# Two column tiles for x_proj in a scan-plus-experts kernel, and an earlier due time for steps that give a PSUM bank back

## Chip, cores, metric

The kernel runs on one core of a Trainium2 chip. Its time is the device time of one execution in microseconds (us), as the median of the runs. All data are fp32.

## What is computed

Two layers work on x of shape (8, 384, 32, 32), with 1024 tokens per image. Layer 0 is a selective-scan block with a GELU MLP behind it; layer 1 is a mixture of four experts. Each has a group norm ahead and a residual around it. Cut to what matters:

```python
# layer 0, per image, t = tokens x channels (1024 x 384), after group norm and layer norm
xm, z = split(t @ in_proj_w.T)                    # 768 + 768
xc = silu(conv3(xm))                              # causal, 3 taps per channel
dbc = xc @ x_proj_w.T                             # 768 -> 24 + 16 + 16
dt, Bm, Cm = split(dbc, [24, 40])
dt = softplus(dt @ dt_proj_w.T + dt_proj_b)       # 24 -> 768
h_t = exp(dt*A) * h_(t-1) + (dt*xc) * Bm          # 16 states per channel, a scan over tokens
y = (sum_n h * Cm + xc * D) * silu(z)
x1 = x + gelu((y @ out_proj_w.T) @ w1.T + b1) @ w2.T + b2
# layer 1
out = x1 + sum_e coef_e * (relu(gn(x1) @ W1_e + b1_e) @ W2_e + b2_e)   # e = 0..3, two of them nonzero per token
```

The step that the change rewrites is `dbc = xc @ x_proj_w.T`: 768 inputs (six blocks of 128), 56 outputs.

## The kernel before

The tokens are cut into 16 chunks of T = 512, two to an image. Channels lie on the 128 partitions. A chunk of the scan has 24 rounds (6 blocks d of 128 channels, 4 groups s of states). In a round ScalarE makes four decays (`decay`, L790), GpSimd the drive (`drive`, L798), VectorE four scans (`scan`, L806), VectorE and GpSimd multiply the states by C (`read_out`, L810), and TensorE adds them over states into the PSUM tile y (`sum_states`, L832): four matmuls of 32 output columns side by side in the array, one per `tile_position`. Each fp32 matmul appears in the trace as two matmul instructions.

Around the scan of chunk i, the same engines do the dense work of its neighbours: in_proj and conv (L319, L338, L339), gate (L357) and x_proj (L378 to L396) of chunk i+1, out_proj (L500), the MLP (`hidden` L521, `second` L561) of chunks before, the scores of layer 1 (`scores`, L608) and the experts' first layer (`expert_lane`, L663), whose results go to DRAM. When the last scan is done, what is left of this dense work is finished, and then the experts' second layer runs for all chunks (L1147), 576 matmuls one after another.

The order of instructions is not written out by hand. A planner (`run`, `issue_one`, L938 to L976) walks through a modelled time at build time, with a clock per engine, and issues one step after another. The rounds of the scan are chains of `Step`s with dependences. The dense work consists of `Task`s, Python generators that yield an engine and a modelled duration for each step. On an engine, in this order, goes a side step that is late (`overdue`, L877: 2*(1+rank) us after it became ready, and 25 us more for a batch with table loads); then a due step of the scan; then a side step that fits into a gap (`fits`). On TensorE nothing counts as late. The plan fixes the order per engine, and the engines then wait for each other by semaphores.

Dense results go to one pool of four PSUM banks (`bank`, `free`, L211 to L216; BANKS = 4). A step that begins a matmul group in a fresh bank is issued only while fewer than four are held (L941). The bank is given back behind the step that empties it: an eviction by ScalarE or VectorE (`evict`, L482; `expert_evict`, L670), or the second of conv's two VectorE steps.

x_proj (L378) is planned at round 9 of the chunk before (L998). It takes a bank at its first matmul, adds the six blocks into rows 0 to 55 of it, one matmul per step, waits until the last dt projection of the chunk before is made (L387; the tile dbc has one buffer), copies the sum to SBUF on ScalarE (L391), gives the bank back and writes rows 24 to 55 to DRAM, from where they are read back spread over partitions (`load_rows`). The conv results come in two batches of SiLU, planned at rounds 6 and 9: blocks 0 to 2, and blocks 3 to 5. `delta` (L427) makes dt of one channel block out of dbc and is due from round 15 on.

Of the kernel before, what the change touches and what calls it, by code (L numbers as in the profile page):

```python
# [13 lines left out]
ALU = mybir.AluOpType  # L14
# [4 lines left out]
P = 128  # L19
# [6 lines left out]
ND = DI // P  # L26
# [5 lines left out]
BANKS = 4  # L32
# [3 lines left out]
MM, SUMS = 0.91, 1.05  # L36
ACT, COPY, TABLES = 0.70, 0.60, 2.6
SCAN, READ_A, DVE = 1.22, 1.30, 0.74
# [2 lines left out]
LAG = 0.07  # L41
SLACK = {"DVE": 0.35, "ACT": 0.15, "POOL": 0.3}
BATCH_SLACK = 0.5
RANK = 16.0
POLL = 0.5
DTR = 24
# [74 lines left out]
def layers(ctx, tc, io, ident, cmean, eps, dram, x1_dram, gn1, logits, r_dram, group_norm):  # L121
# [7 lines left out]
    V, S, G, PE = nc.vector, nc.scalar, nc.gpsimd, nc.tensor  # L129
# [27 lines left out]
    def weight(name, shape, queue=S):  # L157
        t = wp.tile(shape, F32, name="w_" + name)
        queue.dma_start(t, io[name])
        return t  # L160
# [5 lines left out]
    w_x = weight("x_proj", [P, ND, DTR + 2 * NS])  # L166
# [33 lines left out]
    xc, zs, dtr, dxr, dbc, bc_dram, bt, ct, gn = {}, {}, {}, {}, {}, {}, {}, {}, {}  # L200
# [5 lines left out]
    psq_user = []  # L206


    held = [0]

    def bank(name):  # L211
        held[0] += 1
        return ps_g.tile([P, T], F32, name=name, tag="g")

    def free():
        held[0] -= 1  # L216

    class Stream:

# [158 lines left out]
    def x_proj(i):  # L378
        g = None
        m = DTR + 2 * NS  # L380
        for d in range(ND):
            while (i, d) not in xc:
                yield "-", POLL
            yield "bank" if d == 0 else "PE", MM
            g = bank("g_x") if d == 0 else g
            PE.matmul(g[0:m, :], lhsT=w_x[:, d, :], rhs=xc[i, d], start=(d == 0), stop=(d == ND - 1))
        while i > 0 and (i - 1, ND - 1) not in projected:  # L387
            yield "-", POLL
        yield "ACT", COPY
        sums = p1.tile([m, T], F32, name="dbc")  # L390
        S.copy(sums, g[0:m, :])  # L391
        yield "-", 0
        free()
        bc_dram[i] = dram.tile([2 * NS, T], F32, name=f"bc_dram{i}")
        nc.sync.dma_start(bc_dram[i], sums[DTR:m, :])
        dbc[i] = sums  # L396
# [14 lines left out]
    def load_b(i, s):  # L411
        begin(load("b", bt, i, 0, s), rank=0)
# [66 lines left out]
    tt, x1, hs, pre, ready = {}, {}, {}, {}, {}  # L479
    scored, waiting = set(), set()  # L480

    def evict(g, us, engine, then, done=lambda: None):  # L482
        yield engine, us
        then(g)
        yield "-", 0
        free()
        done()

    def out_proj(i):
        while (i, ND - 1) not in finished or i - 1 in tt:  # L490
            yield "-", POLL
        t = p1.tile([P, J, T], F32, name="tt")
        for j in range(J):
            g = None
            for k in range(2):
                yield "bank" if k == 0 else "PE", 3 * MM
                w = w_out.take("out_proj", 2 * j + k)
                g = bank("g_out") if k == 0 else g
                for d in range(3):
                    PE.matmul(g, lhsT=w[:, d, :], rhs=xc[i, 3 * k + d], start=(k + d == 0), stop=(k == 1 and d == 2))  # L500

            begin(evict(g, COPY, "ACT", lambda g, j=j: S.copy(t[:, j, :], g),
                        lambda j=j: ready.setdefault(i, []).append(j)), rank=1, after=now[0] + 3 * MM)
        yield "-", 0
        out_done.add(i)
        while len(ready.get(i, [])) < J:
            yield "-", POLL
        tt[i] = t

    def hidden(i, us):  # L510
        while i not in tt:
            yield "-", POLL
        for u in us:
            while len(waiting) == HID:
                yield "-", POLL
            yield "bank", 3 * MM
            waiting.add((i, u))
            w = w_1.take("mlp_w1", u)
            g = bank("hid")
            for j in range(J):  # L520
                PE.matmul(g, lhsT=w[:, j, :], rhs=tt[i][:, j, :], start=(j == 0), stop=(j == J - 1))  # L521

            def then(g, u=u):
                h = pre[i, u] = ph.tile([P, T], F32, name="h")
                S.activation(h, g, AF.Identity, bias=b1[:, u:u + 1])
            begin(evict(g, ACT, "ACT", then), rank=1, after=now[0] + 3 * MM)
            if u % 3 == 2:
                begin(gelus(i, range(u - 2, u + 1)))

# [19 lines left out]
    def second(i, half):  # L549
        us = range(half * NF // 2, (half + 1) * NF // 2)  # L550
        for j in range(J):
            g = None
            for k in range(2):
                mine = [(i, us[3 * k + n]) for n in range(3)]
                while not all(m in hs for m in mine) or i not in x1:
                    yield "-", POLL
                yield "bank" if k == 0 else "PE", 3 * MM
                w = w_2.take("mlp_w2", 4 * j + 2 * half + k)
                g = bank("acc") if k == 0 else g
                for n in range(3):  # L560
                    PE.matmul(g, lhsT=w[:, n, :], rhs=hs[mine[n]], start=(k + n == 0), stop=(k == 1 and n == 2))  # L561

            def then(g, j=j):
                y = x1[i][:, j, :]
                if half == 0:
                    V.scalar_tensor_tensor(y, g, b2[:, j:j + 1], y, ALU.add, ALU.add)
                    return
                V.tensor_tensor(y, g, y, ALU.add)
                b = i // NH
                if b not in stats:  # L570
                    stats[b] = p2.tile([P, NH * J, 6], F32, name="st1")
                V.bn_stats(stats[b][:, (i % NH) * J + j, :], y)
                summed[i] = summed.get(i, 0) + 1
                if summed[i] == J:
                    nc.sync.dma_start(x1_dram[i], x1[i])
                    if i % NH == NH - 1:
                        begin(scores(i // NH))
            begin(evict(g, 2 * DVE if half else DVE, "DVE", then), rank=1, after=now[0] + 3 * MM)
        yield "-", 0
        waiting.difference_update((i, u) for u in us)  # L580

# [68 lines left out]
    def expert_lane():  # L650

        for i in range(NCH):
            if i < NCH - 1:
                yield from load_xn(i, pxn)
            while i not in xns:
                yield "-", POLL
            xn = xns.pop(i)
            for u in range(E * J):
                yield "bank", 3 * MM
                w = w_e.take("e_w1", u)  # L660
                h = bank("e_hid")
                for j in range(J):
                    PE.matmul(h, lhsT=w[:, j, :], rhs=xn[:, j, :], start=(j == 0), stop=(j == J - 1))  # L663

                begin(expert_evict(h, i, u), rank=1, after=now[0] + 3 * MM)
            yield "-", 0

    writing = []
# [1 line left out]
    def expert_evict(h, i, u):  # L670
        while len(writing) == 2:
            yield "-", POLL
        writing.append((i, u))
        yield "ACT", ACT
        r = pr.tile([P, T], F32, name="r")
        S.activation(r, h, AF.Relu, bias=e_b1[:, u:u + 1])  # L676
        yield "-", 0
        free()
        nc.sync.dma_start(r_dram[i][u], r)
        yield "-", DMA  # L680
        writing.remove((i, u))
# [174 lines left out]
    class Task:  # L856
        def __init__(self, steps, rank, after):
            self.steps, self.rank, self.end, self.engine = steps, rank, after, None
            self.advance()

        def advance(self):
            last = self.engine
            self.engine, us = next(self.steps, (None, 0))
            self.at = "PE" if self.engine == "bank" else "ACT" if self.engine == "batch" else self.engine
            self.us = us
            self.ready = self.end + (us if self.engine == "-" else 0) + (LAG if self.engine != last else 0)
# [7 lines left out]
        def urgency(self):  # L874
            return self.rank * RANK + self.ready

        def overdue(self):  # L877
            return self.ready + 2 * (1 + self.rank) + (25 if self.engine == "batch" else 0)

    now, clock = [0.0], {"PE": 0.0, "DVE": 0.0, "ACT": 0.0, "POOL": 0.0}  # L880
    tasks, ends, steps, chains = [], {}, {}, {e: [] for e in clock}

    def begin(*new, rank=2, after=None):
        tasks.extend(Task(t, rank, now[0] if after is None else after) for t in new)

    def chain(engine, items):

# [37 lines left out]
    def fits(t):  # L925
# [9 lines left out]
        wait = max(0, now[0] - t.ready) if t.engine == "batch" else 0  # L935
        return end + ACT + 2 * LAG <= starved() + (BATCH_SLACK + wait / 10 if t.engine == "batch" else 0)

# [294 lines left out]
```

## Time and profile before

| | us |
|---|---|
| median of 3 runs (lowest, highest) | 3879.05 (3877.36, 3880.08) |
| the profiled execution's own time | 3874.76 |
| its span | 3873.0 |
| mean granted TensorE clock | 0.965 |
| x_proj's 96 matmuls (L386): busy | 95.4 |
| the sums over states (L832), 384 groups of four: busy | 462.9 |
| copies dbc<-g_x (L391), 16 | 9.1 |
| the experts' second layer (L1147), 576 matmuls: busy | 494.6 |

Busy time is the time in which an engine works, on a row or in a window. "Idle before, releaser" tells what an engine's next instruction waited for. TensorE's ends are modelled, so the distance from one start to the next is the better measure there. A share of busy time is a mean over stages with different limits, so it is read by stage.

### The profile page before, as it was taken

What the parts mean: (1) busy time and instruction counts of PE and PEld (TensorE: products, weight loads), DVE (VectorE), ACT (ScalarE), POOL (GpSimd) and SP (SyncE); (2) the same over time, 40 slices, a digit from 0 to 9 for tenths busy, and PEclk for the clock granted to TensorE, in tenths of its full rate; (3) what the DMA queues carried; (4) which work ended last, traced back from release to release, by engine and by line L of the source; (5) the groups of instructions that cost most, each with busy time, mean ns of one, the idle gap of its engine ahead of it and who ended that gap; (6) DMA issues with size and microseconds to landing.
All of it is one profiled execution on the core that took longest, in us unless ns stands there. A gap on an engine that the chain in (4) does not pass through costs nothing.

```text
span 3873.0 us, 35214 instructions
## 1 busy us (share of the span) xinstructions
PE 3628.0 (94%) x10294; PEld 1374.8 (35%) x10294; DVE 3008.6 (78%) x3081; ACT 2385.4 (62%) x3714; POOL 2773.1 (72%) x1070
## 2 busy tenths in 40 slices
PE   6769798999999999999999999999999998999999
PEld 2213233333333333333333333333333343444444
DVE  3899899999989998989799979898888802055554
ACT  4758586868787878787777777777776632200000
POOL 2899899999989998999899989899889800000000
PEclk8869898999999999999999999999999998999999
DMA  4334455555546565555555456555555536555553
GB/s 132 123 124 160 150 167 186 169 196 179 202 157 207 179 202 167 202 187 180 177 197 190 162 178 214 174 183 178 179 167 187 177 99 205 199 196 196 187 179 109
DMA packets 374804, 677.90 MB, mean 175 GB/s; under 512 B 40508, under 2 KB 151484, under 8 KB 372436
## 3 DMA queue, kind: packets, MB, share of 16 engines
q1 hardware_dynamic: 372448, 675.31, 52.1%
q8 instruction: 83, 1.36, 0.1%
q14 instruction: 109, 0.89, 0.1%
q10 hardware_dynamic: 2164, 0.34, 0.0%
HBM read 535.90 MB, written 139.59 MB: 174 GB/s over the span
## 4 chain that ended last, share of the span: by engine, by line
PE 49%; DVE 16%; ACT 13%; POOL 9%; DMA 6%; issue 5%; SPq 1%; POOLq 0%; ACTq 0%; DVEq 0%
PE acc L1147 13%; PE e_hid L663 8%; PE acc L561 7%; DVE da_A L806 6%; POOL du L798 6%; PE hid L521 6%; PE g_in L319 6%; DVE du L806 4%; PE y L832 4%; ACT da_A L790 4%; PE g_out L500 4%; POOL du L810 2%; DVE du L810 2%; ACT da_B L790 2%; DMA mlp_w<-in_mlp_w 1%
## 5 line engine op out<-in xcount | busy, mean ns | idle before, releaser
L798 POOL TENSOR_TENSOR du<-dxr,b 128x2048 f32<-128x2048 f32 x384 | 1739.2, 4534 | 84.0 <-PE y L832 56.6
L810 POOL TENSOR_TENSOR du<-du,c 128x1024 f32<-128x1024 f32 x384 | 905.6, 2359 | 114.5 <-DVE du L806 84.5
L790 ACT ACTIVATE da_A<-dtr_a,w_a_log 128x512 f32<-128x512 f32 x768 | 529.5, 689 | 254.0 <-DVE carry L815 106.6
L790 ACT ACTIVATE da_B<-dtr_b,w_a_log 128x512 f32<-128x512 f32 x768 | 525.3, 684 | 217.5 <-DVE du L806 203.9
L319 PE MATMUL g_in<-xt,in_proj 128*128 128x512 f32 x1152 | 554.3, 623 | 44.2 <-DMA in_proj<-in_in_proj 16.9
L663 PE MATMUL e_hid<-xn,e_w 128*128 128x512 f32 x1152 | 534.9, 607 | 36.3 <-DMA xn<-xn_dram 16.0
L521 PE MATMUL hid<-tt,mlp_w 128*128 128x512 f32 x1152 | 536.4, 608 | 27.7 <-DMA mlp_w<-in_mlp_w 22.7
L806 DVE TENSOR_TENSOR_SCAN du<-da_B,carry,du 128x512 f32<-128x512 f32 x384 | 487.6, 1270 | 91.3 <-ACT da_B L790 77.5
L561 PE MATMUL acc<-h,mlp_w 128*128 128x512 f32 x1152 | 541.4, 608 | 17.4 <-DMA mlp_w<-in_mlp_w 10.8
L806 DVE TENSOR_TENSOR_SCAN da_A<-da_A,carry,du 128x512 f32<-128x512 f32 x384 | 491.4, 1280 | 56.9 <-ACT da_A L790 54.1
L832 PE MATMUL y<-du,sel 128*32 128x512 f32 x3072 | 462.9, 625 | 73.5 <-DVE du L810 28.8
L806 DVE TENSOR_TENSOR_SCAN du<-da_B,du 128x512 f32<-128x512 f32 x384 | 464.3, 1209 | 76.4 <-ACT da_B L790 51.0
L806 DVE TENSOR_TENSOR_SCAN da_A<-da_A,du 128x512 f32<-128x512 f32 x384 | 467.7, 1218 | 43.7 <-ACT da_A L790 38.5
L1147 PE MATMUL acc<-r,w_e_w 128*128 128x512 f32 x1152 | 494.6, 592 | 0.0
L810 DVE TENSOR_TENSOR du<-da_A,c 128x1024 f32<-128x1024 f32 x384 | 468.0, 1219 | 8.9
L319 PEld LDWEIGHTS g_in<-xt,in_proj 128*128 128x128 f32 x1152 | 216.9, 196 | 370.6 <-issue 258.1
L663 PEld LDWEIGHTS e_hid<-xn,e_w 128*128 128x128 f32 x1152 | 217.1, 193 | 330.5 <-issue 270.5
L521 PEld LDWEIGHTS hid<-tt,mlp_w 128*128 128x128 f32 x1152 | 214.2, 192 | 330.8 <-issue 276.7
L561 PEld LDWEIGHTS acc<-h,mlp_w 128*128 128x128 f32 x1152 | 213.6, 192 | 323.7 <-issue 277.4
L1147 PEld LDWEIGHTS acc<-r,w_e_w 128*128 128x128 f32 x1152 | 218.9, 190 | 275.5 <-issue 275.5
L500 PE MATMUL g_out<-xc,out_proj 128*128 128x512 f32 x576 | 269.4, 604 | 0.3 <-ACT r L676 0.3
L676 ACT ACTIVATE r<-e_hid,w_e_b 128x512 f32<-128x512 f32 x192 | 129.6, 680 | 194.3 <-PE e_hid L663 127.2
(125 smaller groups left out, 2929.7 us busy)
## 6 DMA issues: line engine op xcount, KB each, us to landing
dxr<-dxr_dram SPq DMA_DIRECT2D x384, 256.0 KB, 4.7
mlp_w<-in_mlp_w SPq DMA_DIRECT2D x384, 192.0 KB, 3.9
dtr_b<-dtr_dram SPq DMA_DIRECT2D x192, 256.0 KB, 4.1
dtr_a<-dtr_dram SPq DMA_DIRECT2D x192, 256.0 KB, 3.3
r_dram<-r SPq DMA_DIRECT2D x192, 256.0 KB, 2.8
r<-r_dram SPq DMA_DIRECT2D x64, 768.0 KB, 4.6
in_proj<-in_in_proj SPq DMA_DIRECT2D x192, 192.0 KB, 3.6
e_w<-in_e_w SPq DMA_DIRECT2D x192, 192.0 KB, 3.5
```

The source lines that it names most:

```text
L319: PE.matmul(g, lhsT=w[:, j, :], rhs=xt[i][:, j, :], start=(j == 0), stop=(j == J - 1))
L500: PE.matmul(g, lhsT=w[:, d, :], rhs=xc[i, 3 * k + d], start=(k + d == 0), stop=(k == 1 and d == 2))
L521: PE.matmul(g, lhsT=w[:, j, :], rhs=tt[i][:, j, :], start=(j == 0), stop=(j == J - 1))
L561: PE.matmul(g, lhsT=w[:, n, :], rhs=hs[mine[n]], start=(k + n == 0), stop=(k == 1 and n == 2))
L663: PE.matmul(h, lhsT=w[:, j, :], rhs=xn[:, j, :], start=(j == 0), stop=(j == J - 1))
L676: S.activation(r, h, AF.Relu, bias=e_b1[:, u:u + 1])
L790: S.activation(out, dtr[i, d][pair][:, j % 2, :], AF.Exp, scale=neg_a[:, d, j, s:s + 1])
L798: G.tensor_tensor(du[r], dxr[i, d], wide(bt[i, s].unsqueeze(1), [P, Q, T]), ALU.mult)
L806: V.tensor_tensor_scan(a if j < 2 else b, a, b, start, ALU.mult, ALU.add)
L810: engine.tensor_tensor(du[r][:, js, :], h, wide(ct[i, s].unsqueeze(1), [P, 2, T]), ALU.mult)
L832: PE.matmul(y[j * m:(j + 1) * m, :], lhsT=sel, rhs=h[:, j, :], start=False, stop=(s == NG - 1), tile_position=(0, j * m), skip_group_check ...
L1147: PE.matmul(acc[j], lhsT=e2[:, e, d, j, :], rhs=r[:, d, :], start=(e + d == 0), stop=(e + d == E + J - 2))
```

## The change

x_proj is done in three pairs of matmuls. Blocks d and d+3 run as two column tiles of one bank: block d into rows 0 to 55 (tile position 0), block d+3 into rows 64 to 119 (tile position 64). A pair is one step with a modelled duration of 1.2 us and starts only when both its blocks are there. The two partial sums are joined behind: ScalarE copies the first to SBUF as before, then a new VectorE step adds the second to it, reading it from PSUM, and the bank is given back after that.

The planner is changed too. A task counts the banks that it holds (`holds`); where one task fills a bank and another empties it, the count is handed on (`current[0].holds -= 1`, `holds=1`). While all four banks are held, a step of a task that holds one is late 0.5 us after it is ready (SHORT), instead of 2*(1+rank) us.

```diff
+SHORT = 0.5
...
-    held = [0]
+    class Nobody:
+        holds = 0
+
+    held, current = [0], [Nobody]
 
     def bank(name):
         held[0] += 1
+        current[0].holds += 1
         return ps_g.tile([P, T], F32, name=name, tag="g")
 
     def free():
         held[0] -= 1
+        current[0].holds -= 1
...
-        for d in range(ND):
-            while (i, d) not in xc:
+
+        for d in range(ND // 2):
+            while (i, d) not in xc or (i, d + ND // 2) not in xc:
                 yield "-", POLL
-            yield "bank" if d == 0 else "PE", MM
+            yield "bank" if d == 0 else "PE", 1.2
             g = bank("g_x") if d == 0 else g
-            PE.matmul(g[0:m, :], lhsT=w_x[:, d, :], rhs=xc[i, d], start=(d == 0), stop=(d == ND - 1))
+            for k in range(2):
+                PE.matmul(g[k * P // 2:k * P // 2 + m, :], lhsT=w_x[:, k * ND // 2 + d, :], rhs=xc[i, k * ND // 2 + d],
+                          start=(d == 0), stop=(d == ND // 2 - 1), tile_position=(0, k * P // 2))
         while i > 0 and (i - 1, ND - 1) not in projected:
             yield "-", POLL
         yield "ACT", COPY
         sums = p1.tile([m, T], F32, name="dbc")
         S.copy(sums, g[0:m, :])
+        yield "DVE", DVE
+        V.tensor_tensor(sums, g[P // 2:P // 2 + m, :], sums, ALU.add)
         yield "-", 0
         free()
...
+            current[0].holds -= 1
             begin(evict(g, COPY, "ACT", lambda g, j=j: S.copy(t[:, j, :], g),
-                        lambda j=j: ready.setdefault(i, []).append(j)), rank=1, after=now[0] + 3 * MM)
+                        lambda j=j: ready.setdefault(i, []).append(j)), rank=1, after=now[0] + 3 * MM, holds=1)
...
         def __init__(self, steps, rank, after):
             self.steps, self.rank, self.end, self.engine = steps, rank, after, None
+            self.holds = 0
             self.advance()
 
         def advance(self):
             last = self.engine
+            outer, current[0] = current[0], self
             self.engine, us = next(self.steps, (None, 0))
+            current[0] = outer
...
         def overdue(self):
+            if self.holds and held[0] == BANKS:
+                return self.ready + SHORT
             return self.ready + 2 * (1 + self.rank) + (25 if self.engine == "batch" else 0)
...
-    def begin(*new, rank=2, after=None):
-        tasks.extend(Task(t, rank, now[0] if after is None else after) for t in new)
+    def begin(*new, rank=2, after=None, holds=0):
+        for t in new:
+            tasks.append(Task(t, rank, now[0] if after is None else after))
+            tasks[-1].holds += holds
```

The handing on is done in the same two lines in `hidden`, `second` and `expert_lane`. No other instruction is added or taken away; the order on each engine comes from the planner again.

More of the change, by code (lines that the diff above doesn't have):

```diff
@@ L525, in then @@
                 S.activation(h, g, AF.Identity, bias=b1[:, u:u + 1])
-            begin(evict(g, ACT, "ACT", then), rank=1, after=now[0] + 3 * MM)
+            current[0].holds -= 1
+            begin(evict(g, ACT, "ACT", then), rank=1, after=now[0] + 3 * MM, holds=1)
             if u % 3 == 2:
@@ L577, in then @@
                         begin(scores(i // NH))
-            begin(evict(g, 2 * DVE if half else DVE, "DVE", then), rank=1, after=now[0] + 3 * MM)
+            current[0].holds -= 1
+            begin(evict(g, 2 * DVE if half else DVE, "DVE", then), rank=1, after=now[0] + 3 * MM, holds=1)
         yield "-", 0
@@ L663, in expert_lane @@
                     PE.matmul(h, lhsT=w[:, j, :], rhs=xn[:, j, :], start=(j == 0), stop=(j == J - 1))
-                begin(expert_evict(h, i, u), rank=1, after=now[0] + 3 * MM)
+                current[0].holds -= 1
+                begin(expert_evict(h, i, u), rank=1, after=now[0] + 3 * MM, holds=1)
             yield "-", 0
```

## Prediction, made blind

> **What bounds the kernel now.** I read the busy shares first, then cut the span into stages at the points where the work changes, then took TensorE's waits by stage, then single instructions. The stages (columns: window in us, its length, then busy us and count of each engine, granted clock, DMA share, GB/s):
>
> ```profile
> 0.00:700.00 700.00, 567.71 (x1565) 190.41 (x1566) 581.18 (x601) 475.94 (x758) 590.40 (x245) 0.87 0.46 150
> 700.00:3090.00 2390.00, 2306.24 (x6973) 852.21 (x6972) 2135.97 (x2125) 1830.97 (x2840) 2182.53 (x825) 0.99 0.55 184
> 3090.00:3373.00 283.00, 259.45 (x606) 113.47 (x606) 29.51 (x58) 77.76 (x116) 0.20 (x1) 0.95 0.48 157
> 3373.00:3873.00 500.00, 494.57 (x1153) 218.69 (x1151) 261.97 (x299) 0.69 (x1) 0.00 (x0) 1.00 0.50 179
> ```
>
> To 700 us the scan leads: GpSimd and VectorE are busy and TensorE idles 132 us, because the dense work of later layers isn't there yet. From 700 to 3090 TensorE is busy 96.5%; VectorE idles 254 us. From 3090, where the last sum over states ends, TensorE alone works off what is left of the MLP and the experts' first layer, and from 3373 the experts' second layer. So after 700 us a microsecond of TensorE work is nearly a microsecond of span, wherever the planner puts it. Its waits between 700 and 3090 (us in total, times, longest):
>
> ```profile
> PE hid L521 <- DMA mlp_w<-in_mlp_w: 22.7, 10, 5.7
> PE acc L561 <- DMA mlp_w<-in_mlp_w: 6.7, 5, 2.6
> PE g_in L319 <- ACT da_B L790: 6.4, 3, 2.9
> PE mu L281 <- ACT r L676: 4.7, 2, 3.1
> PE y L832 <- POOL du L810: 4.4, 5, 1.5
> ```
>
> All lines of this view together come to 84 us: 37 for DMAs, 8.5 of y for the scan, 38 of dense matmuls for a ScalarE or VectorE step, mostly one that gives back a bank or makes an input. TensorE hardly waits for the scan here. It is the other way round, in GpSimd's waits of the same window:
>
> ```profile
> POOL du L810 <- DVE du L806: 74.1, 44, 6.2
> POOL du L798 <- PE y L832: 52.2, 27, 6.3
> ```
>
> The second line is the scan held up by TensorE.
>
> **What a matmul costs**, from TensorE's timeline (start, length, engine, line; two instructions are one fp32 matmul):
>
> ```profile
> 1499.83 1.92 PE L386 MATMUL g_x<-xc,w_x_proj 128*56 128x512 f32 x4
> 1501.68 1.06 PE L832 MATMUL y<-du,sel 128*32 128x512 f32 x8
> 1502.68 1.07 PE L386 MATMUL g_x<-xc,w_x_proj 128*56 128x512 f32 x2
> 1503.67 5.42 PE L521 MATMUL hid<-tt,mlp_w 128*128 128x512 f32 x12
> 1509.02 1.06 PE L832 MATMUL y<-du,sel 128*32 128x512 f32 x8
> ```
>
> From start to start, two x_proj matmuls take 1.85, one takes 0.99: 0.86 each and 0.13 once per group. Four y matmuls in four column tiles take 1.00, as much as one x_proj matmul. Six 128-column matmuls take 5.35. The last stage gives the bare price, 494.6/576 = 0.859.
>
> **Part 1, x_proj in pairs.** Removed: six matmuls in a row per chunk, 6 x 0.86. Added: three pairs. No row shows two tiles of 64 columns. The bounds are the y row (tiles run fully side by side: 0.86 a pair) and two x_proj matmuls (no overlap: 1.72). I take 0.86, since y runs four tiles with four moving tensors in that time. That is 3 x 0.86 = 2.58 us less per chunk, 41 in all.
>
> [...] The row: a group in another mode costs 0.13 at its end, and three dense matmuls take 2.67 instead of 2.58 ahead of a y, 0.09 at its start; together 0.22. [...] But the x_proj of before pays the 0.13 already. In the instruction order, which is fixed at build time, its 96 matmuls stand in 53 groups; the 48 pairs stand in 32. Counted over all kinds, TensorE changes between kinds 922 times before the last y in the old order and 887 times in the new, 35 x 0.12 = 4 us less. I take the row.
>
> x_proj of chunks 0 to 3 lies ahead of 700 us, where TensorE waits for the scan. Those 4 x 2.58 = 10 us only turn into idle. What counts is 31 + 4 = 35 us.
>
> **Part 2, the VectorE add.** Nearest row: x<-acc,x (L568), a sum of PSUM and SBUF into SBUF, 676 ns; 16 x 0.68 = 11 us on VectorE, covered by its 254 us of idle time. If that cover is gone it is 11 on the path. The add also waits for ScalarE's copy, and scans are queued behind it. VectorE's longest wait for a decay here is 5.0 us, so I bound this at 0 to 16 x 3 = 48, and take 0 beyond the 11, as the planner puts the add behind the copy's planned end. For what follows, the copy stands near round 14.2 of the chunk before (15.2 in the old order) and the first dt near round 16: 1.8 rounds of 7.8 us cover 0.7 us, and the write of B and C and their loads on SP's queue come no later. Only chunk 0 at the start has no cover: 0.7 us.
>
> **Part 3, banks.** Pairs need blocks 3 to 5, so x_proj's bank is taken at round 12 instead of 9 to 11, and given back at 14 to 15 instead of 14 to 16. One bank of four is held for about 2 rounds rather than 4 to 5. With SHORT, evictions go ahead of scan steps while all four are held. Both let the planner fit in more dense work before the scan ends. Behind the last y the old order has 285 dense matmuls (18 out_proj, 45 hid, 57 acc, 165 e_hid), the new one 186 (18, 36, 36, 96). So 99 x 0.859 = 85 us of work goes out of the stage 3090 to 3373 and into the scan's stage.
>
> *Stage behind the scan:* -85, if its idle time stays. TensorE waits 23.4 us there, for xn (12.0) and e_w (11.4). In the new order no expert group stands between hid and acc of the last half, nor beside the group norm's small matmuls, as some do now: about 2.7 for a GELU batch with its table load, and 10 to 12 from the last acc over statistics, norm and logits. But then e_hid of chunks 14 and 15 starts when xn lands, about when it does now, and the wait for e_w behind the big loads lies inside that. I take the same 23; bounds 10 and 45.
>
> *Scan's stage, 700 to 3090:* TensorE's load goes from 2306 to 2306 + 85 - 35 = 2356. Idle time on top: 37 for DMAs and 8.5 for the scan stay; of the 38 for banks and inputs I let half go, 19. That makes 2421, +31. With none gone +50; with all gone +12.
>
> *What the late rule may cost:* ScalarE's side work between two decays is lumpier in the new order. Summed over the rows' durations, what exceeds 4 us between two decays comes to 205 us instead of 168, with ten lumps of 8 to 13 us against one. Decays feed scans, so up to 37 us go onto the scan chain. The scan's own pace is 184 to 187 us per chunk where it leads (drives before 700 us), 12.5 chunks make 2300 to 2340; with 37 it is 2340 to 2377, still under 2421. So I put it at nothing beyond the idle time kept above; without that cover it is 37.
>
> **Sum** on the profiled execution: 31 - 85 + 0.7 = -53. Span 3873 - 53 = 3820, own time 3821.6 (1.8 lie around the span). The median of the runs is 4.3 above that execution's own time, so I predict 3826.
>
> **Rivals.**
> - *More absorbed:* most bank waits go, the scan's stage grows by 12 or less: -73 and beyond, under 3806. For it: the shorter hold, and chunks that take 192 to 199 us while TensorE idles up to 8% in some 100 us slices. Against it: mlp_w's 29 us come from DMA and nothing here changes them. 0.16.
> - *Lumps or unoverlapped tiles eat part:* the 37 us come on top of TensorE's load (-53 + 37 = -16, 3863), or pairs cost 1.72 (-53 + 31 = -22, 3857). The y row speaks against the second. Between 3845 and 3871: 0.17.
> - *Slower:* one mechanism, the eviction lumps on ScalarE at the conv and SiLU batches of each chunk (rounds 8 to 16). A lump starves VectorE's scans, the sums over states come late, and TensorE, in order, stands before y with dense work queued behind, as it does before 700 us. Price: 50 of load with no idle saved, 37 of lumps, 11 of the add: 98 on the scan's stage, against 85 gained: +13, 3892. It decides from 85 us of growth, 6.8 us per chunk. For it: VectorE waits 186 us for decays already. Against it: y waits for the scan only 8.5 us there, so the scan has room. 0.09.
>
> **How the numbers follow.** The likeliest case, 3806 to 3845, has 0.54 and gives 3826. About 0.2% (8 us) is what a measurement can tell from no change; 3871 to 3887 gets 0.04. Faster is 0.54 + 0.16 + 0.17 = 0.87, slower 0.09. The range from 3788 to 3868 leaves out 0.06 below (all idle for banks gone and a tail with 10 of waits) and 0.14 above.
>
> **What would show it.** Right: L386's successor has 96 matmuls with about 50 us busy, 3 pairs start to start in 2.7; the last y ends near 3120, the experts' second layer starts near 3320; dense waits for ScalarE and VectorE about 19 between 700 and the last y. Wrong: pairs at 1.7; y waiting tens of us for GpSimd or VectorE after 700 (slower rival); the stage behind the scan longer than 210 us, which would mean that the chain of the last chunk is bare.

## The result and the profile after

| | before | after |
|---|---|---|
| median us (lowest, highest), 4 runs each | 3878.2 (3877.11, 3880.08) | 3820.39 (3816.69, 3823.5) |
| ratio, 95% interval | | 0.985 (0.9833 to 0.9867) |
| span of the profiled execution | 3873.0 | 3816.7 |
| TensorE busy / span less busy | 3628.0 / 245.0 | 3586.5 / 230.2 |
| x_proj's matmuls, busy | 95.4 | 53.9 |
| last y starts; experts' second layer starts | 3088.8; 3373.0 | 3123.4; 3316.7 |

The change gains 58 us; 3820 was measured where 3826 had been predicted. The stages of the changed kernel, cut at the same events (window, length, then busy us and count of TensorE's matmuls, its weight loads, VectorE, ScalarE, GpSimd; granted clock, DMA share, GB/s):

```profile
0.00:700.00 700.00, 558.34 (x1537) 187.95 (x1538) 577.48 (x597) 467.55 (x745) 579.66 (x242) 0.86 0.45 147
700.00:3124.00 2424.00, 2357.83 (x7198) 882.29 (x7196) 2157.32 (x2151) 1852.72 (x2884) 2195.33 (x828) 0.99 0.57 188
3124.00:3317.00 193.00, 176.07 (x417) 77.47 (x410) 24.72 (x51) 56.51 (x86) 0.21 (x1) 0.93 0.46 153
3317.00:3817.00 500.00, 494.24 (x1152) 218.50 (x1150) 262.00 (x299) 0.69 (x1) 0.00 (x0) 1.00 0.50 179
```

The scan's stage has grown by 35 us and carries 52 us more TensorE work; the stage behind it has shrunk from 283 to 193; the last is the same. The pairs, in TensorE's timeline (start, length; four instructions are one pair):

```profile
1707.19 1.07 PE L394 MATMUL g_x<-xc,w_x_proj 128*56 128x512 f32 x4
1708.19 1.07 PE L847 MATMUL y<-du,sel 128*32 128x512 f32 x8
1709.19 1.12 PE L444 MATMUL g_dt<-dbc,w_dt_proj 24*128 24x512 f32 x2
1710.24 1.93 PE L394 MATMUL g_x<-xc,w_x_proj 128*56 128x512 f32 x8
1712.10 1.12 PE L325 MATMUL g_in<-xt,in_proj 128*128 128x512 f32 x2
```

One pair takes 1.00 from start to start and two take 1.86, where one and two single matmuls took 0.99 and 1.85: the two tiles run side by side. Of TensorE's waits from 700 us to the last y, the longest:

```profile
PE e_hid L677 <- DMA e_w<-in_e_w: 14.4, 5, 3.6
PE acc L574 <- DMA mlp_w<-in_mlp_w: 5.7, 5, 2.0
PE y L847 <- ACT y L840: 5.0, 4, 1.8
PE g_x L394 <- ACT z L363: 4.8, 1, 4.8
PE g_logits L635 <- ACT h L537: 3.7, 1, 3.7
```

All lines of this view come to 66 us (84 before): 23 for DMAs (37), 10.6 of y (8.5), 32 for ScalarE and VectorE (38). y's waits have grown by 2 us only, so the scan keeps up. And behind the last y, the longest:

```profile
PE e_hid L677 <- DMA xn<-xn_dram: 6.6, 1, 6.6
PE g_logits L635 <- ACT x L628: 2.7, 2, 1.8
PE acc L574 <- ACT h L549: 2.7, 1, 2.7
PE gn_m L100 <- DVE gn_mv L97: 1.9, 1, 1.9
```

The last chunk's chain, which had expert groups in its gaps before, now shows its waits, but they are small: 17 us in this stage against 23.

### The profile page after: what moved, and what is told of

It reads as the page before. It is cut to its first block, busy times and chain, and to the rows that moved or that the text cites. A ratio compares the mean times of both kernels' runs of the same rounds, so it can differ in the third digit from the quotient of the medians.

```text
span 3816.7 us, 35175 instructions
## 1 busy us (share of the span) xinstructions
PE 3586.5 (94%) x10294; PEld 1366.2 (36%) x10294; DVE 3021.5 (79%) x3097; ACT 2377.5 (62%) x3714; POOL 2775.2 (73%) x1070
## 4 chain that ended last, share of the span: by engine, by line
PE 49%; DVE 17%; ACT 15%; POOL 7%; issue 5%; DMA 5%; SPq 2%; ACTq 0%; POOLq 0%; DVEq 0%
PE acc L1169 13%; PE e_hid L677 8%; DVE da_A L821 7%; PE hid L533 7%; PE acc L574 6%; PE g_in L325 6%; POOL du L813 5%; DVE du L821 5%; PE y L847 4%; ACT da_A L805 4%; PE g_out L511 3%; DVE du L825 2%; POOL du L825 2%; ACT da_B L805 2%; ACT L205 2%
## 5 line engine op out<-in xcount | busy, mean ns | idle before, releaser
L533 PE MATMUL hid<-tt,mlp_w 128*128 128x512 f32 x1152 | 528.2, 603 | 14.0 <-DMA mlp_w<-in_mlp_w 7.1
L847 PEld LDWEIGHTS y<-du,sel 128*32 128x32 f32 x3072 | 68.3, 109 | 411.3 <-issue 96.5
```

Source lines behind the costliest of these rows:

```text
L847: PE.matmul(y[j * m:(j + 1) * m, :], lhsT=sel, rhs=h[:, j, :], start=False, stop=(s == NG - 1), tile_position=(0, j * m), skip_group_check ...
```

## The experiments

Every ratio is to the kernel before, run on the same chip. "Idle" is span less TensorE's busy time, in the profiled execution; "rest" is TensorE's busy time without x_proj, the same matmuls in every row. The profiled execution is not always near the median: those of due_only and after_null are 6 us faster, that of one_tile_no_add 6 us slower.

| run | median us | ratio (95% interval) | idle | rest | clock |
|---|---|---|---|---|---|
| before | 3878 | 1 | 245.0 | 3532.6 | 0.965 |
| changed kernel | 3820 | 0.985 (0.9833 to 0.9867) | 230.2 | 3532.6 | 0.966 |
| one_tile | 3838 | 0.9899 (0.9885 to 0.9912) | 224.1 | 3519.6 | 0.969 |
| one_tile_no_add | 3838 | 0.9901 (0.9887 to 0.9914) | 226.4 | 3520.9 | 0.967 |
| due_only | 3848 | 0.9925 (0.9912 to 0.9937) | 220.6 | 3526.1 | 0.967 |
| late_start | 3859 | 0.9957 (0.9944 to 0.9971) | 235.5 | 3527.1 | 0.967 |
| pairs_only | 3870 | 0.9979 (0.9971 to 0.9987) | 263.6 | 3549.1 | 0.962 |
| pairs_only_null | 3857 | 0.9947 (0.9935 to 0.996) | 249.8 | 3549.8 | 0.962 |
| short_2 | 3830 | 0.9882 (0.9868 to 0.9895) | 233.0 | 3537.7 | 0.963 |
| three_held | 3856 | 0.9948 (0.9935 to 0.996) | 259.5 | 3541.6 | 0.962 |
| after_null | 3827 | 0.9874 (0.9859 to 0.9889) | 230.2 | 3534.2 | 0.966 |
| before_null | 3880 | 1.0009 (1.0 to 1.0017) | 249.6 | 3533.0 | 0.966 |
| add_five_psum | 3861 | 0.9959 (0.9945 to 0.9972) | 251.5 | 3555.1 | 0.964 |
| add_five | 3933 | 1.0143 (1.0127 to 1.0158) | 297.1 | 3579.8 | 0.955 |

**one_tile: TensorE's time alone.** The order on all engines is the changed kernel's, instruction for instruction.

```diff
-                PE.matmul(g[k * P // 2:k * P // 2 + m, :], ..., start=(d == 0), stop=(d == ND // 2 - 1), tile_position=(0, k * P // 2))
+                PE.matmul(g[0:m, :], ..., start=(d + k == 0), stop=(d + k == ND // 2))
-        V.tensor_tensor(sums, g[P // 2:P // 2 + m, :], sums, ALU.add)
+        V.tensor_tensor(sums, g[0:m, :], sums, ALU.max)
```

> The plan and the order are those of the changed kernel, but each pair's two matmuls go into the same column tile, one behind the other, and VectorE's step reads that tile again (a maximum of equal values, the same duration). Only TensorE's time per pair differs. Theory A (after 700 us TensorE's work is the span; a pair saves 0.86): 12 chunks x 2.58 = 31 us slower than the changed kernel, 3851, with x_proj busy about 95. Theory B (the gain comes from the order and the banks, and the time saved on TensorE falls into its waits): 0 to 10 us slower, 3820 to 3830.

0.49% or 19 us slower than the changed kernel, between the two theories. x_proj's group and the scan's stage:

```profile
L394 PE MATMUL g_x<-xc,w_x_proj 128*56 128x512 f32 x192 | 92.6, 618 | 12.6 <-ACT xc L379 4.9 <-ACT z L363 4.1 <-ACT h L537 3.6
```

```profile
700.00:3141.00 2441.00, 2383.77 (x7194) 889.53 (x7196) 2157.80 (x2151) 1854.34 (x2883) 2195.28 (x828) 0.99 0.56 187
```

x_proj costs 38.7 us more here, yet the span is only 19.6 longer (3836.3 against 3816.7). The order is the same, so the two executions can be compared at one and the same matmul. Near 700 us (the changed kernel first):

```profile
699.64 2.74 PE L677 MATMUL e_hid<-xn,e_w 128*128 128x512 f32 x6
699.73 2.74 PE L677 MATMUL e_hid<-xn,e_w 128*128 128x512 f32 x6
```

Up to there the tiles have saved 7.3 us of x_proj and gained nothing, as the prediction said for the stage in which the scan leads; the other matmuls took 10 us longer there, at a clock of 0.86 instead of 0.87. Behind it they save 31.4 us. Of these, 17.5 have arrived at the last y (3123.4 against 3140.9) and 19.6 at the end. Before the last y, 9 us have become idle time (66.2 against 57.2; the waits for ScalarE and VectorE are 32 against 26), and the other matmuls take 5 us longer.

**due_only and late_start: the order alone.** due_only is the changed kernel with x_proj as before. late_start is the kernel before, with this edit:

```diff
-            while (i, d) not in xc:
+            while (i, d) not in xc or (i, ND - 1) not in xc:
```

> The late rule with SHORT, with x_proj as before (six matmuls, no add). It leaves 213 dense matmuls behind the last y. Theory A: TensorE has as much to do as before, so only waits can go: 10 to 20 us faster than before, 3858 to 3868. Theory B: 72/99 of 58 us, 42 us, 3836.

> x_proj as before (one tile, six matmuls, old late rule), but its first matmul waits until all six blocks are there, as the first pair nearly does, so that its bank is held for two or three rounds instead of five. It leaves 270 dense matmuls behind the last y, and x_proj stands in 38 groups instead of 53. Theory A: 15 x 0.2 = 3 us from fewer groups and a few us of waits, 3870 to 3876. Theory B: 15/99 of 58, 9 us, 3869, or more if the held bank was the cause of the waits.

due_only gains 0.75%, 29 us, more than theory A allows and less than B. late_start gains 0.43%, 17 us, with the same six matmuls: more than A allows and than the 9 us of B, which left room for more if the held bank was the cause. In the traces x_proj's bank is held for 27.0 us in the mean before, from the first matmul to the end of the step that empties it; for 13.1 in late_start, 14.1 in the changed kernel and 32.1 in due_only. TensorE's waits for ScalarE and VectorE fall from 38 to 26 us in late_start, which is what a bank that is free sooner would do; how much of the 17 is an accident of the new order is not shown (see before_null below). one_tile, which has both the rule and the late start, gains 39; the two tiles make it 58.

**pairs_only: the pairs without the rule,** and its twin with a pair planned 0.02 us shorter.

```diff
-            if self.holds and held[0] == BANKS:
-                return self.ready + SHORT
```

> The pairs and the VectorE add, with the late rule of before (no SHORT). Behind the last y it leaves 249 dense matmuls (285 before, 186 in the changed kernel). Theory A: 31 to 35 us from TensorE's time and nothing from waits, 3843 to 3847. Theory B, in which the gain goes with what the plan packs into the scan: 36/99 of 58 us, 21 us, 3857.

> As pairs_only (the late rule of before), with a pair's modelled duration 1.18 instead of 1.20 us. It leaves 204 dense matmuls behind the last y, where pairs_only leaves 249. If pairs_only's small gain of 8 us belongs to the pairs without the rule: again 3862 to 3872. If it is an accident of its order: 3838 to 3850, as TensorE's time alone would give.

Theory A fails here: 40 us are off x_proj, but only 8 and 20 off the time. The stages of pairs_only:

```profile
700.00:3121.00 2421.00, 2324.96 (x7047) 860.65 (x7049) 2150.16 (x2145) 1843.55 (x2867) 2195.07 (x828) 0.98 0.56 184
3121.00:3367.00 246.00, 226.07 (x541) 99.41 (x534) 28.91 (x57) 66.90 (x101) 0.21 (x1) 0.95 0.47 158
```

TensorE idles 96 us in the first window (84 before): 47 for ScalarE and VectorE steps (38), 20 of y for the scan (8.5), 28 for DMAs (37). The clock is 0.98 (0.99 before), and over the whole run the other matmuls take 16.5 us longer. The planner left 249 matmuls behind the scan. What the pairs saved went into waits, the scan's among them, and into slower matmuls. The twin leaves 204 matmuls and still gains only 20, so the smallness isn't just an accident of one order; the 12 us between the two are. A pair waits for both its blocks, so pairs_only has the late start too (15.5 us of hold), which alone gained 17: without the rule, the faster matmuls added nothing to it that can be told from such accidents.

**before_null and after_null: what an accident of the order is worth.**

```diff
-            yield "bank" if d == 0 else "PE", MM          # before_null
+            yield "bank" if d == 0 else "PE", MM + 0.02
-            yield "bank" if d == 0 else "PE", 1.2         # after_null
+            yield "bank" if d == 0 else "PE", 1.18
```

> The kernel before, with x_proj's modelled duration 0.02 us longer per matmul. Nothing else is changed, but the planner's order shifts throughout: it leaves 300 dense matmuls behind the last y instead of 285. This measures what an accident of the order is worth. If orders of one rule are worth the same: within 4 us of before, 3872 to 3880. If the accident is as large as what pairs_only (8 us) and late_start (17 us) gained: 10 us or more away, either way.

> The changed kernel, with a pair's modelled duration 1.18 instead of 1.20 us. It leaves 177 dense matmuls behind the last y instead of 186. If orders of one rule are worth the same: within 4 us of the changed kernel, 3814 to 3824. If the accident of the order is large: 10 us or more away, either way.

3.5 and 9 us: a planned duration that moves by 0.02 us shifts the whole order and the time by up to 0.3%. Only the 12 us of pairs_only and its twin are clear of the intervals; those of the changed kernel and after_null overlap, and before_null's reaches 1. So differences between kernels of different orders are uncertain by some 10 us, whatever their intervals; one_tile, one_tile_no_add and the two add runs keep the order and are free of that.

**short_2 and three_held: the strength of the rule.** `SHORT = 2.0`, and `held[0] >= BANKS - 1` instead of `held[0] == BANKS`.

> The changed kernel with SHORT = 2.0, between its 0.5 and the 4 us of most evictions in the old rule. It leaves 198 dense matmuls behind the last y. If the rule works by its strength: between pairs_only and the changed kernel, 3825 to 3845. If any hurry of this order is enough: as the changed kernel, 3815 to 3828.

> The changed kernel, with the short late rule already at three held banks. It leaves 171 dense matmuls behind the last y (186 in the changed kernel). If evictions are what TensorE still waits for (32 us in the changed kernel): 5 to 20 us faster than it, 3800 to 3815. If evictions put ahead of scan steps cost the scan: y waits for the scan more than 10.6 us, and it is as fast or slower, 3820 to 3835.

Without the rule 3857 to 3870, with 2.0 us 3830, with 0.5 us 3820 to 3827, from three banks on 3856. So 2.0 and 0.5 us can't be told apart, but the rule can be too strong. three_held has the fewest matmuls left behind the scan of all (171) and few waits for ScalarE and VectorE steps (15 us), but TensorE's waits in the scan's stage now begin with y:

```profile
PE y L847 <- DVE du L825: 13.9, 7, 4.4
PE e_hid L677 <- DMA xn<-xn_dram: 10.1, 3, 5.0
PE e_hid L677 <- DMA dtr_b<-dtr_dram: 6.1, 1, 6.1
PE g_in L325 <- DMA in_proj<-in_in_proj: 6.0, 5, 2.6
PE y L847 <- POOL du L825: 6.0, 3, 2.5
```

All y waits there come to 29 us (10.6 in the changed kernel), and ScalarE's side work beyond 4 us between two decays to 253 us, counted in the instruction order with the rows' durations (205 in the changed kernel, 168 before). This fits the mechanism of the slower rival, one step further on; that the lumps make the y waits is argued, not shown.

**The add.** add_five and add_five_psum put four more VectorE operations behind it, and one_tile_no_add takes the one of one_tile away.

```diff
+        for _ in range(4):
+            V.tensor_tensor(sums, sums, sums, ALU.max)                                              # add_five
+            V.scalar_tensor_tensor(sums, g[P // 2:P // 2 + m, :], 0.0, sums, ALU.mult, ALU.add)     # add_five_psum
-        V.tensor_tensor(sums, g[0:m, :], sums, ALU.max)                                             # one_tile_no_add
```

> The changed kernel in its own order, with four more VectorE operations of the same size behind x_proj's add (a maximum of equal values that changes nothing): 64 more, about 0.69 us each, 44 us on VectorE, and dbc 2.8 us later in each chunk. If the add is covered by VectorE's idle time: 0 to 8 us slower than the changed kernel. If VectorE's scans are on the path there: 30 to 44 us slower; the single add then cost 8 to 11 us.

> As add_five, but the four added VectorE operations per chunk read the second partial sum from PSUM (0 times it, added to the sum: nothing changes), as the add of the change does. 64 more of about 0.73 us, 47 us on VectorE. In add_five the added operations with both inputs in SBUF took 1.86 us in the mean and up to 4.9, and it came out 112 us slower than the changed kernel. If VectorE's own time is what costs: 100 us or more slower than the changed kernel again. If the waits for GpSimd did: all at 0.73 us and 0 to 47 us slower; the single add is then 0 to 12 us.

> As one_tile (the changed kernel's order, one column tile), with VectorE's step after x_proj left empty, so that 16 operations of 0.69 us are gone and the bank and dbc are free that much earlier. Against one_tile (3838): 0 to 3 us faster if VectorE's idle time covers the add, 11 us faster (3827) if it lies on the path.

add_five is 2.9% slower than the changed kernel, 114 us for 64 operations. Its groups show that it measured something else than VectorE's time:

```profile
L404 DVE TENSOR_TENSOR dbc<-dbc 56x512 f32<-56x512 f32 x64 | 118.9, 1859 | 2.2
L402 DVE TENSOR_TENSOR dbc<-g_x,dbc 56x512 f32<-56x512 f32 x16 | 11.1, 693 | 11.5 <-ACT dbc L400 11.2
```

With both inputs in SBUF these operations take 1859 ns in the mean: the shortest 682, the median 684, the longest 4924. With one input in PSUM it is 693. The timeline of one place:

```profile
2974.05 0.69 DVE L402 TENSOR_TENSOR dbc<-g_x,dbc 56x512 f32<-56x512 f32 x1
2974.77 12.59 DVE L404 TENSOR_TENSOR dbc<-dbc 56x512 f32<-56x512 f32 x4
2975.28 1.72 POOL L462 TENSOR_TENSOR dtx<-dt,xc 128x512 f32<-128x512 f32 x1
2976.96 9.85 POOL L815 TENSOR_TENSOR du<-dxr,b 128x2048 f32<-128x2048 f32 x2
```

Four operations, 0.68 us each at the shortest, take 12.59 us together here, while three of GpSimd run (1.72 and two drives, 4.9 each where 4.5 is usual). The last of the four starts at 2982.5 and ends at 2987.36, 0.55 us after the second drive. The longest such operation is 4.92 us, about as long as a drive there. That VectorE waits there until GpSimd's instruction is done fits these lengths; what makes it wait the runs don't show. The add of the change reads one side from PSUM and takes 692 to 694 ns in all 16. In add_five_psum, where the four more read that side too, they take 692 in the mean:

```profile
L404 DVE SCALAR_TENSOR_TENSOR dbc<-g_x,dbc 56x512 f32<-56x512 f32 x64 | 44.3, 692 | 2.2
```

It is 1.1% (42 us) slower than the changed kernel for these 44.3 us. Compared at the same matmul, it is 13 us behind the changed kernel at 700 us and 43 at the last y, so the loss builds up all through the scan. one_tile_no_add equals one_tile (0.9901 and 0.9899). So the first 11 us of VectorE time are covered, to within some 8 us, and the next 44 are not. The add was taken away with TensorE as slow as before; for the changed kernel itself that it is covered is not shown. Whether they cost by VectorE's time or because four in a row keep dbc and the bank for 2.8 us longer, these runs don't tell.

## Why the prediction was right, and where not

The time, its direction and its stages came as worked out: the last y at 3123 (3120 predicted), the experts' second layer at 3317 (3320), x_proj's busy time at 54 (50), 193 us behind the scan (under 210).

- *A pair costs 0.86, as in the y row*: right. Where TensorE goes from one kind of matmul to another ("another mode" in the prediction), it costs what the row said: 0.14 at the end of a group of pairs (1.00 and 1.86 against 0.86 and 1.72), and three dense matmuls ahead of a pair take 2.67 against 2.58 (1704.52 to 1707.19). What TensorE does in that time is not shown.
- *The add is covered*: right in one_tile, shown by taking it away. "Covered by its 254 us of idle time" does not hold as a reason: 44 us more cost 42.
- *85 us move out of the stage behind the scan, and its idle time stays*: nearly right, -91: 83 to 85 us of work, and 7 us of idle time besides (17 instead of 23). The 2.7 for a GELU batch was measured at 2.7. The norm and the logits came to 6.8 in place of 10 to 12.
- *31 + 4 us of TensorE's time come off the scan's stage*: mis-sized. The matmul time is right: at a fixed order the tiles save 31 us behind 700 us. But only 18 to 20 of them reach the time. The sum carried matmul time into the span one to one and left idle time as it was; idle time grew by 9 in that stage.
- *Half of the 38 us for banks and inputs goes, DVE and ScalarE waits fall to 19*: failed as stated. They fell only to 32, while DMA waits, which "nothing here changes", fell from 37 to 23: those for mlp_w from 29 to 8, those for e_w rising from 1 to 14. So the order of the steps matters to them too; how, no run here isolates. The total idle time, 66, agrees with the 64.5 of the sum by luck of two terms.
- *The order (rule and shorter hold)*: under-sized. one_tile against before is 39 us without a faster matmul. In the sum it stood for 19 of idle time. The two errors, -16 in one term and +20 in the other, cancel; that 3826 was near 3820 is luck to that extent.
- *Lumps cost nothing*: holds as far as the profile shows it. VectorE waits 182 us for decays (186 before), though the longest wait grew from 5.0 to 8.6. In three_held y waits for the scan 29 us.

Theory A (TensorE's work is the span) and theory B (the gain goes with what the plan packs into the scan) both fall: the gain does not follow the count left behind the scan either (171 left, 20 us; 204, 20; 213, 29; 186, 58). What stands: the span is TensorE's busy time plus its idle time, and a change has to be followed through both. What stays open is how much of the 29 us of the rule alone, and of the 17 of the late start, is its own and how much an accident of some 10 us. No version among these was faster than the changed kernel.

## What to carry to other kernels

Even in a stage where the bounding engine idled under 4%, removing its work paid only in part, and 9 us of it came back as idle time; change one thing at a fixed instruction order to learn the exchange rate, here 18 to 20 us of 31 in that stage, and none of 7 ahead of it. With a planner that writes the order, run a null variant first: a planned duration off by 0.02 us moved the time by up to 12 us, so a gain of that size says nothing about the edit. A shared bank that is taken late and given back soon came with a gain (17 us) about as large as that of the faster matmuls (19), though the first number carries the 10 us of an accident and the second doesn't.

## What the runs showed of the hardware

In these runs, where TensorE idles more, the same matmuls tend to take longer as well. The other matmuls (column "rest") take 3520 to 3526 us in the three runs that idle 221 to 226 us, 3527 to 3538 in the five at 230 to 245, 3533 to 3555 in the five at 250 to 264 and 3580 in the one at 297, with the mean granted clock at 0.967 to 0.969 at the one end and 0.955 at the other. It is no strict rule: the kernel before and the changed one differ by 15 us of idle time and agree in this column. The kernel before shows it on the small:

```profile
1070.00:1080.00 10.00, 10.00 (x34) 4.64 (x36) 9.64 (x10) 9.66 (x17) 9.24 (x3) 1.00 0.51 162
1080.00:1090.00 10.00, 7.70 (x18) 3.02 (x19) 9.96 (x11) 9.07 (x15) 8.69 (x4) 0.66 0.34 124
```

```profile
1083.27 5.32 PE L319 MATMUL g_in<-xt,in_proj 128*128 128x512 f32 x6 [2.30 <-ACT logits L635]
1088.43 2.74 PE L521 MATMUL hid<-tt,mlp_w 128*128 128x512 f32 x6
1091.10 1.07 PE L832 MATMUL y<-du,sel 128*32 128x512 f32 x8
```

In the second slice TensorE is idle for 2.30 us and its clock is 0.66 in the mean; from 1081.5 to 1088.3 us it is 0.50, before and after that 1.00. The three dense matmuls behind the gap take 5.16 us from start to start, the next three 2.67: the gap comes with about 2.5 us beyond itself. In this trace's clock records between 700 us and the last y, the clock falls to 0.50 eleven times, six times for 3.4 us and five times for 6.8; each time a gap of 1.86 to 5.74 us in TensorE's work lies over the start or ends at most 1.5 us ahead of it, in nine cases under 3.1 us. Five other gaps of 2.3 to 3.3 us have no such fall, so the length alone does not decide; what does is not shown.
